# Sparse attention over 2,708 nodes on one Trainium2 core: sum the late rows of h at their pair of q, seven natural tiles and no natural pair

## The chip, the cores and the metric

The kernel runs on one NeuronCore of a Trainium2 chip. The metric is the device time of one execution in microseconds (us); lower is better. Before the change three executions took 743.93, 744.54 and 748.93 us, so the median is 744.54 us. The profiled execution is a further one.

## The reference

`x` is 2708 x 1024, `adj` is a 2708 x 2708 matrix of zeros and ones with a one in about 0.15% of its places (some four per row), the three weights are 1024 x 1024, all float32.

```python
h = jnp.maximum(_layernorm(x, axis=-1), 0.0)
q = h @ W_q.T + b_q
k = h @ W_k.T + b_k
v = h @ W_v.T + b_v
z = (1.0 / math.sqrt(1024)) * (q @ k.T)
spare_z = z * adj
spare_z = jnp.where(spare_z == 0.0, -10000.0, spare_z)
attn = softmax(spare_z, axis=1)
return x + relu(attn @ v)
```

## The kernel before, in words

**The algebra.** The kernel never forms k or v. It multiplies the two weights once into a matrix M, so that a row of `q` (h times M plus a bias) has to be multiplied only with rows of h. For each node it finds its neighbours in `adj`, gathers their rows of h, takes one dot product for each, makes softmax weights of them, and sums the gathered rows into a row u. The output is x + relu(u times W_v plus bias). A node with no edge has equal weights on all nodes, so its u needs the sum of all rows of h (`hsum`).

**Sorting and slots.** Rows are handled in 21 full tiles of 128 rows and a rest of 20. Nodes are sorted by how many neighbours they have, in two parts: the first EARLY tiles, and all others. In a sorted part, tile t needs only K[t] slots (gathers, dot products, sums), from 15 in its first tile to 2 in its last. With EARLY = 9 the slots are 15 7 6 5 4 4 3 3 2 | 15 7 6 6 5 5 4 4 3 3 2 2, in all 111. The tiles that may hold nodes without an edge are EMPTY = (8, 20).

**Stage one** (0 to about 200 us). M is made of 256 matmuls in four parts (`part_of_m`, L340), while ScalarE and VectorE apply the layernorm (`stats`, `root`, `apply`: letters s, r, a in `follow`, L233) and search `adj` (`edges`, L246: letter e). ScalarE's order is written out by hand here: the strings given to `follow` are issued on it in that order, ahead of the evictions that come after them in the code. `apply` also adds each tile to `hsum` on VectorE (L229) and writes it to `h_dram`.

**Natural tiles** (about 128 to 236 us). `query` (L289) forms q of tiles 0 to 6 in natural order, 16 matmuls each. In the middle of tile 4 (`mid`) stands `sort` (L458): two matmuls that count degrees, a few VectorE operations that give every node its place (`pos_i`, L493), and then on GpSimd the writes of one row of a table per node (`put`, L436, one indirect DMA for a tile): first the tiles EARLY to 21, then a load of the sorted table, then two gathers of sorted rows of h (`first_rows`), then the tiles 0 to EARLY - 1, their load, and two more gathers. Tiles 7 and 8 are a natural pair: they are loaded from `h_dram` in order, and `query` of tile 6 stands around their transposes.

**Units.** From here TensorE runs 17 units of two tiles: units 0 to 6 form q of the pairs (7,8), (9,10) to (19,20), units 7 to 16 multiply u with W_v for the pairs in `o_pairs`. A unit is seven products of four matmuls (`multiply`, L754, by a scheme of Strassen's kind with 7 instead of 8 products) and, in between, the 16 transposes of the next unit's rows (`blocks`, L504). VectorE makes four sums s1 to s4 for the next unit (L515) and takes two of the results out of PSUM (L800 and L803 in a q unit, L825 and L829 in an o unit); ScalarE takes out the others.

**The attention stream.** The generator `attention` (L697) yields, tile after tile in the list `order`, dot products (L633), weights (L674 to L677) and sums (L685), all on VectorE in one chain. `advance` weaves it into the units: after each of the seven products, a seventh of 21 us of stream work in a q unit and of 20 in an o unit, from unit 1 on; where the next o unit needs a tile that is not done, the stream is driven on until it is. Gathers go to 13 slots (11 tiles and two that lie in M), first come first served, on GpSimd's queue, which also loads each tile's sorted q (`fetch`, L602), adds x into the result (L815) and scatters it to the output (L598). A tile's u that is not needed within three units is written to `u_dram` and loaded back by SyncE. q of the tiles 0 to 8 lies in `q_dram`, in natural order, and is gathered; that of the others is written sorted, to `q_late`.

Of the kernel before, what the change touches and what calls it, by code (L numbers as in the profile page):

```python
# [26 lines left out]
TW = 18  # L27
ROWS = 7
HIGH = 11
EMPTY = (8, 20)  # L30
EARLY = 9
SINGLE = 7
NONE = 1e-30
FAR = 20.0
WIDE = 8
# [20 lines left out]
def tile_preln_masked_attention(  # L56
# [131 lines left out]
    def stats(group):  # L188

        G = len(group)  # L190
        mv = stat.tile([P, 4, 2], FT, tag="mv", name="mv")
        if tiles[group[-1]][1] < P:
            nc.vector.memset(mv, 1.0)
        xs = []
        for i, t in enumerate(group):
            t0, n = tiles[t]
            xt = row_tile(f"x_{t}")
            nc.sync.dma_start(xt[:n], x[t0:t0 + n, :])
            st = stat.tile([P, NH, 6], FT, tag="st", name="st")
# [21 lines left out]
    def apply():  # L221

        group, xs, r = normed.pop(0)
        for i, t in enumerate(group):
            t0, n = tiles[t]
            xt = xs[i]
            nc.scalar.activation(xt[:n], xt[:n], AF.Relu, bias=r[:n, 4, i:i + 1], scale=r[:n, 3, i:i + 1])  # L227
            nc.gpsimd.dma_start(h_dram[t0:t0 + n, :], xt[:n])  # L228
            nc.vector.tensor_add(hsum[:n], hsum[:n], xt[:n])  # L229

    normed, adj_loads = [], []

# [56 lines left out]
    def query(hT, banks, name, first=False, between=(), mid=None):  # L289

        q = work.tile([P, D], FT, tag="q", name=f"q_{name}", bufs=4)
        order = [(h, c) for h in range(NH) for c in range(DC)]
        if first:

            order.sort(key=lambda hc: hc[1] >= DC // 2)
        for h, c in order:
            if mid is not None and (h, c) == (1, 3):
                mid(mm)
            mm = nc.tensor.matmul(banks[h], hT[:, c, :], M[:, c // 4, h, c % 4, :], start=False,  # L299
                                  stop=(c == DC - 1), skip_group_check=True)  # L300
        for h in range(NH):
            if h < len(between):
                follow(between[h])
            nc.scalar.copy(q[:, h * NB:(h + 1) * NB], banks[h])
        return q

    ordered = ExitStack()
# [2 lines left out]
    with tc.tile_pool(name="w", bufs=1, side="left") as wp:  # L310
# [45 lines left out]
                                     acc[i].rearrange("q (p j c) -> q j c p", j=2, c=4), AF.Copy, scale=scale)  # L356


        follow("s0-3 e0 r e1 a")
        part_of_m(0, 0, "acc")  # L360
        follow("s4-7 e2")
        part_of_m(0, 1, "tp")
        c_sb = row_tile("c_sb")
        for acc_v, dst in ((acc_c, c_sb), (acc_b, bp_sb)):
# [14 lines left out]

        nc.vector.tensor_scalar(large[:, 0:1], large[:, 0:1], 250000.0 / D, None, op0=ALU.is_gt)  # L380
        nc.vector.tensor_scalar(large[:, 1:2], large[:, 1:2], 10000.0, None, op0=ALU.is_gt)
        follow("r e3 a e4 s8-11 e5 r e6 a s12-13 e7 r e8 a")
        part_of_m(1, 0, "tp")
        h_e = {}
        for t in range(2):
# [39 lines left out]

    def first_rows(n):

        rows_of[n + 1] = [row_tile(f"qr_{t}") for t in (EARLY + 2 * n, EARLY + 2 * n + 1)]
        for k, row in enumerate(rows_of[n + 1]):
            last = gather(row, h_dram[:, :], EARLY + 2 * n + k, SLOTS, P)  # L430
        return last

# [99 lines left out]
                    ("e20 e21", ""))  # L532

    in_t = T.rearrange("p k (a c) w -> p k a (c w)", a=2)
    rows_h = list(h_e.values()) + [in_t[:, k, a, :] for k in (2, 1, 3) for a in range(2)][:SINGLE - 2]
# [6 lines left out]
    for t in range(SINGLE):  # L542
        if t + 2 < SINGLE:
            nc.sync.dma_start(rows_h[t + 2], h_dram[(t + 2) * P:(t + 3) * P, :])
        if t + 1 < SINGLE:
            hT[t + 1] = turned(rows_h[t + 1], f"e{t + 1}")
        ahead_banks = seeded(bp_sb) if t + 1 < SINGLE else None
        if t == SINGLE - 1:

            ops_of = {0: blocks(*rows_of.pop(0))}  # L550
            for part in ops_of[0][1:]:
                part()
        q = query(hT.pop(t), banks, f"e{t}", first=(t == 0), between=work_between[t] if t < 4 else (),
                  mid=sort_here if t == 4 else None)
        nc.scalar.dma_start(q_dram[t * P:(t + 1) * P, :], q)
        banks = ahead_banks
        if t == 3:
            search.close()

            att = ph.enter_context(tc.tile_pool(name="att", bufs=1, side="right", reuse_waits="tile"))  # L560
            slots = []
            for i in range(HIGH):
                slots.append(att.tile([P, D], FT, name=f"g{i}"))


            for c in range(4):
                for k, (i, j) in enumerate(((0, 0), (0, 1), (1, 1), (1, 0))):
                    nc.sync.dma_start(slots[2 * c + k // 2][:, k % 2 * NB:(k % 2 + 1) * NB], wv[j][:, i * 4 + c, :])
            for i in range(8, HIGH):
                nc.gpsimd.memset(slots[i], 0.0)  # L570
        if t == 5:
# [80 lines left out]
    def weights(t):  # L652
# [5 lines left out]
        coef = stat.tile([P, SLOTS], FT, tag="coef", name="coef")  # L658
        u = row_tile(f"u_{t}")
        if t in EMPTY:  # L660
            nc.vector.memset(w[:, 0:1], MASKED)
            nc.vector.tensor_scalar(coef[:, :k], ok, -1.0, -MASKED, op0=ALU.add, op1=ALU.mult)
            nc.vector.tensor_mul(w[:, 1:1 + k], z, ok)
# [61 lines left out]
    chain = [behind[-1]]  # L725
    stream = attention(order)
    spent, now = [0.0], [0]

# [56 lines left out]
    def q_results(ta, tb):  # L785
# [1 line left out]
        qb = work.tile([P, D], FT, tag="q", name=f"q_{tb}", bufs=4)  # L787

        def store(q, t):
            dst = q_dram[t * P:(t + 1) * P, :] if t < EARLY else q_late[(t - EARLY) * P:(t - EARLY + 1) * P, :]  # L790
            nc.sync.dma_start(dst, q)
            formed.add(t)
            if t == EARLY - 1:
                formed.update(range(EARLY))

        def c11(X):
            nc.scalar.copy(qa[:, lo], X)
# [2 lines left out]
            nc.vector.tensor_add(qb[:, hi], Y, p5)  # L800

        def c12(Z, u2):
            nc.vector.tensor_add(qa[:, hi], Z, u2)  # L803
            store(qa, ta)

        def c21(Y):
# [53 lines left out]
        return wv[j][:, i * 4:(i + 1) * 4, :]  # L860


    q_pairs = [(t, t + 1) for t in range(SINGLE, FULL, 2)]
    o_pairs = [(6, 7), (5, 0), (4, 3), (9, 2), (8, 1), (10, 11), (12, 13), (14, 15), (16, 17), (20, 18)]
    alone = 19
    units = [("q",) + p for p in q_pairs] + [("o",) + p for p in o_pairs]
    assert alone == order[-1]

    def load_rows(unit):
        kind, *pair = unit  # L870
# [11 lines left out]
        return rows  # L882

    banks_of = {0: banks_for(bp_sb)}

    for h in range(NH):
# [3 lines left out]
    last_q = len(q_pairs) - 1  # L890
    for n, unit in enumerate(units):
        kind, ta, tb = unit
        now[0] = n
        if 1 <= n <= 3:

            i, j = ((0, 0), (1, 0), (1, 1))[n - 1]
            nc.sync.dma_start(m_dram[i, j], M[:, i, j])
        share = (21.0 if kind == "q" else 20.0) / 7
        nxt = units[n + 1] if n + 1 < len(units) else None
        results = (q_results if kind == "q" else o_results)(ta, tb)  # L900

        def after(i):
            if i in (2, 5):
                send()
            if n:
                advance(share)
            if nxt is not None:

                if i == (0 if n else 4):
                    ops_of[n + 1] = blocks(*rows_of.pop(n + 1))  # L910
# [211 lines left out]
```

## Time and profile before

| | |
|---|---|
| median of three executions | 744.54 us (743.93 to 748.93) |
| profiled execution, its own time | 745.27 us |
| its span in the profile | 743.3 us |
| granted TensorE clock, mean of the core | 0.975 |
| VectorE adds to `hsum`, L229, 128 x 1024 | 21, mean 1210 ns |
| dot products L633, 128 x 1024 | 111, mean 1224 ns |
| sums L685, 128 x 1024 | 92, mean 1283 ns |
| gathers of rows of h for slots, L420 on GpSimd | 125, mean 1239 and 1256 ns |
| table writes L440 on GpSimd | 22, mean 1317 ns |
| gathered pair rows `qr`, from issue to landing | 4.2 least, 5.2 median, 9.7 most (us) |

The page gives busy time of each engine, the span in 40 slices, the DMA queues, the chain of work that ended last, the costliest groups with what ended the idle time before them, and the DMA issues with the time to landing. A line such as `xN | busy, mean | idle before <-releaser` names who was waited for. In the timeline of one engine, neighbouring instructions of one kind are merged, the bracket gives the idle time ahead of them, and a float32 matmul leaves two records, so that x8 is one product of four matmuls.

### The profile page before, as it was taken

To read this page: it belongs to the slowest core of one execution; us is meant where nothing else is said; L and a number is where in the kernel's file an instruction comes from. 1 tells how busy PE (TensorE), PEld (TensorE's weight loads), DVE (VectorE), ACT (ScalarE), POOL (GpSimd) and SP (SyncE) were. 2 spreads that over 40 slices of the span, in tenths; PEclk is the share of its full clock that TensorE was granted. 3 is DMA by queue.
4 is the path that set the end of the run, shared out by engine and by line. 5 is a ranking of instruction groups with operands and counts; after the bars stand their busy time and mean duration, and the time that the engine had idled before them with its cause. 6 is when DMAs were issued, how large, how long until landed. Compare 5 with 4: busy or idle time off the path is not lost.

```text
span 743.3 us, 6402 instructions
## 1 busy us (share of the span) xinstructions
PE 689.6 (93%) x1820; PEld 350.4 (47%) x1820; DVE 522.1 (70%) x1068; ACT 254.4 (34%) x381; POOL 306.8 (41%) x281
## 2 busy tenths in 40 slices
PE   7999998999998996899999987999889999999991
PEld 4776765444444442444444433444434444444440
DVE  6978889898891119889999977987889996012001
ACT  0264658587622222321322222332323334222210
POOL 2010111000184764857773652586566862220221
PEclk9999999999999998999999999899899999999997
DMA  9994999999966395788987998899889876631532
GB/s 352 405 403 167 348 402 341 410 399 388 360 218 215 93 378 166 264 309 281 394 315 261 410 414 357 228 346 278 243 265 244 247 222 177 163 51 63 141 73 85
DMA packets 64019, 202.13 MB, mean 272 GB/s; under 512 B 10010, under 2 KB 10362, under 8 KB 62572
## 3 DMA queue, kind: packets, MB, share of 16 engines
q0 software_dynamic: 34736, 109.77, 45.4%
q1 hardware_dynamic: 26940, 84.04, 30.0%
q10 hardware_dynamic: 2304, 7.87, 2.7%
q8 instruction: 16, 0.26, 0.1%
q14 instruction: 23, 0.19, 0.1%
HBM read 166.62 MB, written 48.61 MB: 290 GB/s over the span
## 4 chain that ended last, share of the span: by engine, by line
DMA 19%; PE 15%; issue 15%; POOL 7%; DVE 6%; ACT 1%; POOLq 0%; DVEq 0%
PE ps L744 7%; PE psy L744 7%; DMA g<-h_dram,tab 6%; POOL g L420 4%; DMA out_dram<-y,tab 4%; DMA pq<-q_late 3%; DVE junk L633 3%; DMA y<-in_x_dram,tab 2%; DVE u L685 2%; DMA qr<-h_dram,tab 2%; DMA u_dram<-u 1%; POOL y L815 1%; DMA pq<-q_dram,tab 1%; DVE s L515 1%; PE pt L270 1%
## 5 line engine op out<-in xcount | busy, mean ns | idle before, releaser
L420 POOL DMA_INDIRECT g<-h_dram,tab x107 | 132.6, 1239 | 56.3 <-issue 20.9
L633 DVE SCALAR_TENSOR_TENSOR junk<-g,pq 128x1024 uint8<-128x1024 f32 x94 | 115.0, 1224 | 42.4 <-DMA pq<-q_dram,tab 22.9
L744 PE MATMUL psy<-T,s 128*128 128x512 f32 x272 | 126.3, 608 | 10.6 <-ACT u L768 6.1
L744 PE MATMUL ps<-M,a 128*128 128x512 f32 x272 | 122.3, 592 | 0.0
L347 PE MATMUL ps_m<-wk,wq 128*128 128x512 f32 x256 | 114.2, 608 | 5.3 <-DMA wq<-in_wq_dram 5.3
L685 DVE SCALAR_TENSOR_TENSOR u<-g,coef,u 128x1024 f32<-128x1024 f32 x79 | 101.4, 1283 | 10.3 <-ACT u L677 7.4
L299 PE MATMUL ps<-M,T_e 128*128 128x512 f32 x224 | 97.8, 593 | 0.7 <-ACT ps L286 0.7
L347 PEld LDWEIGHTS ps_m<-wk,wq 128*128 128x128 f32 x256 | 80.2, 314 | 37.4 <-DMA wk<-in_wk_dram 5.3
L744 PEld LDWEIGHTS psy<-T,s 128*128 128x128 f32 x272 | 52.7, 195 | 79.2 <-issue 65.0
L228 POOL DMA_DIRECT2D h_dram<-x x22 | 11.8, 534 | 169.6 <-ACT x L227 169.0
L744 PE MATMUL psy<-T,a 128*128 128x512 f32 x136 | 67.5, 643 | 13.4 <-DVE p L825 12.1
L744 PEld LDWEIGHTS ps<-M,a 128*128 128x128 f32 x272 | 50.5, 190 | 58.1 <-issue 58.1
L255 DVE FIND_INDEX8 at<-ones,adj 128x8 uint32<-128x685 f32 (+1 forms) x88 | 75.8, 865 | 0.0
L299 PEld LDWEIGHTS ps<-M,T_e 128*128 128x128 f32 x224 | 41.9, 190 | 50.7 <-issue 48.8
L744 PE MATMUL ps<-T,s 128*128 128x512 f32 x136 | 61.2, 592 | 0.0
L744 PE MATMUL ps<-M,s 128*128 128x512 f32 x136 | 61.1, 592 | 0.0
L815 POOL DMA_INDIRECT y<-in_x_dram,tab x21 | 36.7, 1749 | 54.9 <-ACT y L830 32.6
L252 ACT ACTIVATE sized<-adj 128x2708 uint8<-128x2708 f32 (+1 forms) x22 | 54.2, 2465 | 2.1 <-DMA adj<-in_adj_dram 2.0
L515 DVE TENSOR_TENSOR s<-a,pt 128x512 f32<-128x512 f32 x34 | 22.0, 683 | 43.0 <-ACT a L511 43.0
L744 PEld LDWEIGHTS psy<-T,a 128*128 128x128 f32 x136 | 27.3, 206 | 51.2 <-issue 31.8
L598 POOL DMA_INDIRECT out_dram<-y,tab x21 | 24.0, 1143 | 64.9 <-DMA y<-in_x_dram,tab 39.2
L744 PEld LDWEIGHTS ps<-M,s 128*128 128x128 f32 x136 | 25.8, 190 | 32.0 <-issue 32.0
(195 smaller groups left out, 719.6 us busy)
## 6 DMA issues: line engine op xcount, KB each, us to landing
adj<-in_adj_dram SPq DMA_DIRECT2D x21, 1354.0 KB, 11.5
x<-in_x_dram SPq DMA_DIRECT2D x21, 512.0 KB, 9.8
h_dram<-x POOLq DMA_DIRECT2D x21, 512.0 KB, 7.7
u_dram<-u POOLq DMA_DIRECT2D x13, 512.0 KB, 6.4
or<-u_dram SPq DMA_DIRECT2D x13, 512.0 KB, 6.2
q_late<-q SPq DMA_DIRECT2D x12, 512.0 KB, 6.4
pq<-q_late POOLq DMA_DIRECT2D x12, 512.0 KB, 5.0
wq<-in_wq_dram SPq DMA_DIRECT2D x8, 512.0 KB, 8.3
```

Source lines behind the costliest of these rows:

```text
L228: nc.gpsimd.dma_start(h_dram[t0:t0 + n, :], xt[:n])
L252: nc.scalar.activation(sized[:n], a[:n, :, :PW], AF.Abs, accum_out=total[:n, t:t + 1])
L255: nc.vector.max_index(at[:n, g, :], ones[:n, 0:8], a[:n, g, :])
L299: mm = nc.tensor.matmul(banks[h], hT[:, c, :], M[:, c // 4, h, c % 4, :], start=False, stop=(c == DC - 1), skip_group_check=True)
L347: nc.tensor.matmul(acc[i], lhs, wk_sb[o][:, cols], start=(o == 0), stop=(o == DC - 1))
L420: return nc.gpsimd.indirect_dma_start(out=dst, out_offset=None, in_=src, in_offset=off, bounds_check=N - 1, oob_is_err=False)
L515: behind.append(nc.vector.tensor_tensor(ops[name], a, b, op=op))
L598: nc.gpsimd.indirect_dma_start(out=out, out_offset=bass.IndirectOffsetOnAxis(ap=ptab.bitcast(U32)[:n, t, SLOTS:SLOTS + 1], axis=0), in_=y[ ...
L633: chained(lambda: nc.vector.scalar_tensor_tensor(junk, g_of[t][s], 1.0, tq[t], op0=ALU.mult, op1=ALU.mult, accum_out=zall[:, t, s:s + 1]))
L685: chained(lambda: nc.vector.scalar_tensor_tensor(u, g_of[t][s], coef[:, at[t][s]:at[t][s] + 1], u, op0=ALU.mult, op1=ALU.add))
L744: nc.tensor.matmul(bank, a[:, c, :], b[:, c, :], start=False, stop=(c == 3), skip_group_check=True)
L815: nc.gpsimd.indirect_dma_start(out=y[:n], out_offset=None, in_=x, in_offset=off, compute_op=ALU.add)
```

## The change

EARLY becomes 7 and SINGLE goes: the sorted parts are tiles 0 to 6 and 7 to 21, and the slots are 15 7 5 5 4 3 2 | 15 8 6 6 5 5 4 4 4 3 3 3 2 2, again 111. EMPTY becomes (6, 20). There is no natural pair: pair (7, 8) is gathered in sorted order like the others. The rows of the tiles 7 to 20 are no longer added to `hsum` in stage one; each pair's gathered rows are added at its unit (`sum_rows`), the rest of 20 rows at unit 1, and the two matmuls with ones that finish the sum (`all_rows`) move from ahead of unit 0 into unit 5. The table of the late part now has 15 writes ahead of it, not 13, and that of the early part 7, not 9.

ScalarE's hand-written order puts each `r` ahead of a search and gives searches to the places between `r` and `a`. One T (the fourth) is made after the v operands. The stream's first step stands in unit 0 and its first work after unit 0; rows for unit 2 are gathered in unit 0; the shares are 18 and 17 us. `order` and `o_pairs` are new, and tile 6, which may hold nodes without an edge, stands 16th. Four tiles of x use another pool tag.

```diff
-EMPTY = (8, 20)
-EARLY = 9
-SINGLE = 7
+EMPTY = (6, 20)
+EARLY = 7
...
-            xt = row_tile(f"x_{t}")
+            if t in (6, 7, 12, 13):
+                xt = work.tile([P, D], FT, tag="q", name=f"x_{t}", bufs=4)
+            else:
+                xt = row_tile(f"x_{t}")
...
-            nc.vector.tensor_add(hsum[:n], hsum[:n], xt[:n])
+            if t < EARLY:
+                nc.vector.tensor_add(hsum[:n], hsum[:n], xt[:n])
...
-        follow("s0-3 e0 r e1 a")
+        follow("s0-3 r e0 a e1")
         part_of_m(0, 0, "acc")
-        follow("s4-7 e2")
+        follow("s4-7 r e2 a e3")
         part_of_m(0, 1, "tp")
...
-        follow("r e3 a e4 s8-11 e5 r e6 a s12-13 e7 r e8 a")
+        follow("s8-11 r e4 a e5 s12-13 e6 r e7 a e8")
         part_of_m(1, 0, "tp")
...
-        rows_of[n + 1] = [row_tile(f"qr_{t}") for t in (EARLY + 2 * n, EARLY + 2 * n + 1)]
-        for k, row in enumerate(rows_of[n + 1]):
+        rows_of[n] = [row_tile(f"qr_{t}") for t in (EARLY + 2 * n, EARLY + 2 * n + 1)]
+        for k, row in enumerate(rows_of[n]):
...
-        if t == SINGLE - 1:
-
-            ops_of = {0: blocks(*rows_of.pop(0))}
-            for part in ops_of[0][1:]:
-                part()
...
-            rows_of[0] = [row_tile(f"h_e{k}") for k in range(SINGLE, EARLY)]
-            for k, row in enumerate(rows_of[0], SINGLE):
-                nc.sync.dma_start(row, h_dram[k * P:(k + 1) * P, :])
...
-        ts_of_m(0, 2, 1, 3)
+        ts_of_m(0, 2, 1)
...
+        ts_of_m(3)
...
+        fill()
+        yield 0.0
...
-    formed = set()
-    order = [6, 7, 5, 0, 4, 3, 9, 2, 8, 1, 10, 11, 12, 13, 14, 15, 16, 17, 18, 20, 19]
+    formed = set(range(EARLY))
+    order = [5, 4, 3, 0, 2, 1, 7, 8, 9, 10, 11, 12, 13, 14, 15, 6, 16, 17, 20, 18, 19]
...
-    for h in range(NH):
-        ps_h = psum.tile([P, NB], FT, tag="tp", name="ps_h")
-        nc.tensor.matmul(ps_h, ones, hsum[:, h * NB:(h + 1) * NB], start=True, stop=True)
-        nc.scalar.copy(hsum[:, h * NB:(h + 1) * NB], ps_h)
+    def sum_rows(rows, n=P):
+        with tc.issue_after(behind[-1].ins):
+            for row in rows:
+                nc.vector.tensor_add(hsum[:n], hsum[:n], row[:n])
...
-        share = (21.0 if kind == "q" else 20.0) / 7
+        share = (18.0 if kind == "q" else 17.0) / 7
...
-            if n:
+            if n == 0 and i == 2:
+
+                next(stream)
...
+            if n or i > 5:
                 advance(share)
...
+                    rows = rows_of.pop(n + 1)
+                    if nxt[0] == "q":
+                        sum_rows(rows)
+                    if n == last_q - 1:
+                        all_rows()
...
-                if i == 4 and n and n + 2 < len(units):
+                if i == 4 and n == 1:
+                    rest = row_tile("h_rest")
+                    gather(rest[:REST], h_dram[:, :], FULL, SLOTS, REST)
+                    sum_rows([rest], REST)
+                if i == 4 and n + 2 < len(units):
```

More of the change, by code (lines that the diff above doesn't have):

```diff
@@ L295, in query, with evict @@
             order.sort(key=lambda hc: hc[1] >= DC // 2)
+        def evict(h):
+            if h < len(between):
+                follow(between[h])
+            nc.scalar.copy(q[:, h * NB:(h + 1) * NB], banks[h])
         for h, c in order:
             if mid is not None and (h, c) == (1, 3):
+                evict(0)
                 mid(mm)
@@ L300, in query @@
                                   stop=(c == DC - 1), skip_group_check=True)
-        for h in range(NH):
-            if h < len(between):
-                follow(between[h])
-            nc.scalar.copy(q[:, h * NB:(h + 1) * NB], banks[h])
+        for h in range(NH) if mid is None else (1,):
+            evict(h)
         return q
@@ L534, in tile_preln_masked_attention @@
     in_t = T.rearrange("p k (a c) w -> p k a (c w)", a=2)
-    rows_h = list(h_e.values()) + [in_t[:, k, a, :] for k in (2, 1, 3) for a in range(2)][:SINGLE - 2]
+    rows_h = list(h_e.values()) + [in_t[:, k, a, :] for k in (2, 1, 3) for a in range(2)][:EARLY - 2]
     placed = []
@@ L540, in sort_here @@
             placed.append(sort())
-    for t in range(SINGLE):
-        if t + 2 < SINGLE:
+    for t in range(EARLY):
+        if t + 2 < EARLY:
             nc.sync.dma_start(rows_h[t + 2], h_dram[(t + 2) * P:(t + 3) * P, :])
-        if t + 1 < SINGLE:
+        if t + 1 < EARLY:
             hT[t + 1] = turned(rows_h[t + 1], f"e{t + 1}")
-        ahead_banks = seeded(bp_sb) if t + 1 < SINGLE else None
-        if t == SINGLE - 1:
-            ops_of = {0: blocks(*rows_of.pop(0))}
-            for part in ops_of[0][1:]:
-                part()
+        ahead_banks = seeded(bp_sb) if t + 1 < EARLY else None
         q = query(hT.pop(t), banks, f"e{t}", first=(t == 0), between=work_between[t] if t < 4 else (),
@@ L660, in weights @@
         if t in EMPTY:
+            assert summed
             nc.vector.memset(w[:, 0:1], MASKED)
@@ L721, in tile_preln_masked_attention @@
     done, held, at, ws, us = set(), {}, {}, {}, {}
-    formed = set()
-    order = [6, 7, 5, 0, 4, 3, 9, 2, 8, 1, 10, 11, 12, 13, 14, 15, 16, 17, 18, 20, 19]
+    formed = set(range(EARLY))
+    order = [5, 4, 3, 0, 2, 1, 7, 8, 9, 10, 11, 12, 13, 14, 15, 6, 16, 17, 20, 18, 19]
     assert sorted(order) == list(range(FULL))
-    chain = [behind[-1]]
+    chain = [placed[0]]
     stream = attention(order)
@@ L789, in store @@
         def store(q, t):
-            dst = q_dram[t * P:(t + 1) * P, :] if t < EARLY else q_late[(t - EARLY) * P:(t - EARLY + 1) * P, :]
-            nc.sync.dma_start(dst, q)
+            nc.sync.dma_start(q_late[(t - EARLY) * P:(t - EARLY + 1) * P, :], q)
             formed.add(t)
-            if t == EARLY - 1:
-                formed.update(range(EARLY))
         def c11(X):
@@ L802, in c12 @@
         def c12(Z, u2):
-            nc.vector.tensor_add(qa[:, hi], Z, u2)
+            behind.append(nc.vector.tensor_add(qa[:, hi], Z, u2))
             store(qa, ta)
@@ L860, in of_wv @@
         return wv[j][:, i * 4:(i + 1) * 4, :]
-    q_pairs = [(t, t + 1) for t in range(SINGLE, FULL, 2)]
-    o_pairs = [(6, 7), (5, 0), (4, 3), (9, 2), (8, 1), (10, 11), (12, 13), (14, 15), (16, 17), (20, 18)]
-    alone = 19
+    q_pairs = [(t, t + 1) for t in range(EARLY, FULL, 2)]
+    o_pairs = [(order[i], order[i + 1]) for i in range(0, FULL - 1, 2)]
+    alone = order[-1]
     units = [("q",) + p for p in q_pairs] + [("o",) + p for p in o_pairs]
-    assert alone == order[-1]
     def load_rows(unit):
@@ L884, in tile_preln_masked_attention, with all_rows @@
     banks_of = {0: banks_for(bp_sb)}
-    for h in range(NH):
-        ps_h = psum.tile([P, NB], FT, tag="tp", name="ps_h")
-        nc.tensor.matmul(ps_h, ones, hsum[:, h * NB:(h + 1) * NB], start=True, stop=True)
-        nc.scalar.copy(hsum[:, h * NB:(h + 1) * NB], ps_h)
     last_q = len(q_pairs) - 1
+    summed = []
+    def sum_rows(rows, n=P):
+        with tc.issue_after(behind[-1].ins):
+            for row in rows:
+                nc.vector.tensor_add(hsum[:n], hsum[:n], row[:n])
+    def all_rows():
+        for h in range(NH):
+            ps_h = psum.tile([P, NB], FT, tag="tp", name="ps_h")
+            nc.tensor.matmul(ps_h, ones, hsum[:, h * NB:(h + 1) * NB], start=True, stop=True)
+            nc.scalar.copy(hsum[:, h * NB:(h + 1) * NB], ps_h)
+        summed.append(True)
+    ops_of = {0: blocks(*rows_of[0])}
+    for part in ops_of[0][1:]:
+        part()
+    sum_rows(rows_of.pop(0))
+    chain.append(behind[-1])
     for n, unit in enumerate(units):
@@ L904, in after @@
                 send()
-            if n:
+            if n == 0 and i == 2:
+                next(stream)
+            if n == 0 and i == 6:
+                chain.append(behind[-1])
+            if n or i > 5:
                 advance(share)
             if nxt is not None:
-                if i == (0 if n else 4):
-                    ops_of[n + 1] = blocks(*rows_of.pop(n + 1))
+                if i == (0 if n else 3):
+                    ops_of[n + 1] = blocks(*rows_of[n + 1])
                     ops_of[n + 1][1]()
```

## The prediction

> **What bounds the kernel now.** I read the page first, then TensorE's timeline from 100 us on, then GpSimd's and VectorE's around 200 to 300 us, then the waits. On the page, the rows of the 40 slices (18.6 us each):
>
> ```profile
> span 743.3 us, 6402 instructions
> ...
> PE 689.6 (93%) x1820; PEld 350.4 (47%) x1820; DVE 522.1 (70%) x1068; ACT 254.4 (34%) x381; POOL 306.8 (41%) x281
> ...
> PE   7999998999998996899999987999889999999991
> ...
> DVE  6978889898891119889999977987889996012001
> ...
> DMA  9994999999966395788987998899889876631532
> ```
>
> TensorE is busy or waiting in order; it lacks 53.7 us in all (743.3 - 689.6). VectorE is full until slice 12 (220 us), almost empty in slices 13 to 15, and full again until 620 us. So two things set the end: TensorE's own work, and in units 2 to 13 VectorE. TensorE's timeline gives the places of the missing time; the bracket is the idle time ahead, with who ended it:
>
> ```profile
> 114.09 1.21 PE L270 MATMUL pt<-ident,h_e 128*128 128x128 f32 x8 [3.29 <-issue]
> 231.30 1.06 PE L270 MATMUL pt<-ident,h_e 128*128 128x128 f32 x8 [1.89 <-DMA h_e<-h_dram]
> 237.37 3.60 PE L744 MATMUL ps<-M,a 128*128 128x512 f32 x8
> 284.90 5.73 PE L744 MATMUL psy<-T,s 128*128 128x512 f32 x8 [6.10 <-ACT u L768]
> 298.36 3.60 PE L744 MATMUL ps<-M,a 128*128 128x512 f32 x8
> 304.49 1.06 PE L270 MATMUL pt<-ident,qr 128*128 128x128 f32 x8 [2.53 <-DMA qr<-h_dram,tab]
> 442.22 5.40 PE L744 MATMUL psy<-T,s 128*128 128x512 f32 x8 [3.29 <-ACT psy L760]
> 464.00 6.63 PE L744 MATMUL psy<-T,a 128*128 128x512 f32 x8 [5.21 <-DVE p L825]
> 522.44 6.42 PE L744 MATMUL psy<-T,a 128*128 128x512 f32 x8 [3.67 <-DVE p L825]
> 637.09 3.60 PE L744 MATMUL ps<-M,a 128*128 128x512 f32 x8
> ```
>
> The lines at 237.37, 298.36 and 637.09 are the starts of units 0, 2 and 14. Units 3 and 4 start at 326.87 and 352.65, so a unit without a wait takes 25.8 us. From unit 14 on nothing waits: 106.2 us to the end, fixed. Units 0 and 1 took 60.99 instead of 51.6 us, units 2 to 13 took 338.7 instead of 309.6.
>
> The hand-over from natural tiles to units hangs on GpSimd's queue and then on VectorE:
>
> ```profile
> 203.78 0.18 DVE L493 CAST pos_i<-deg 128x22 uint32<-128x22 f32 x1
> ...
> 227.31 0.89 POOL L440 DMA_INDIRECT tab_dram<-tab,pos_i  x1 [0.30 <-issue]
> 233.52 1.12 POOL L447 DMA_DIRECT2D tab<-tab_dram  x1 [5.32 <-DMA tab_dram<-tab,pos_i]
> 237.44 1.02 POOL L422 DMA_INDIRECT qr<-h_dram,tab  x1 [2.24 <-DMA tab<-tab_dram]
> 238.77 0.97 POOL L422 DMA_INDIRECT qr<-h_dram,tab  x1 [0.30 <-issue]
> ...
> 280.37 1.23 DVE L633 SCALAR_TENSOR_TENSOR junk<-g,pq 128x1024 uint8<-128x1024 f32 x1 [17.65 <-DMA pq<-q_dram,tab]
> ```
>
> From `pos_i` to the first gathered pair are 34 us of GpSimd's queue; today the natural pair covers them for TensorE. The first dot product starts only at 280.37, because 13 slot gathers stand ahead of the gather of q and that gather needs the natural pair's stores.
>
> **What the Trainium skill says.** "TensorE: Matmul & The Clock Gate", Part 1: The HAM clock gate, says that the array falls to half its clock after an idle window of about 3.4 us and needs about as long of work to come back. This trace agrees: after waits of 3.3 to 6.1 us eight records took 5.40 to 6.63 us, not 3.60. "SBUF — State Buffer", SBUF: two separate sides, says that GpSimd, and with it the descriptors of its DMAs, can be blocked by VectorE on a shared port. Here a table write took 1.50 to 2.83 us until VectorE's subtractions ended at 223 us, and 0.89 to 0.96 after. "DMA: Bandwidth & Descriptors", Issuing engines are not separate DMA queues, says that all issuers share 16 DMA engines. At 405 to 460 us, when SyncE loads the v operands, their share is 1.02 and a gather lands up to 21.9 us after issue (median 6.6).
>
> **Part 1, stage one.** Fifteen adds of 1.21 us leave VectorE (18.2 us), but TensorE waits there only 3.29 us at 114.09 (the eviction L355 stood on ScalarE behind `apply`, which waited 6.81 us for VectorE's r) and about 1.3 us in three small places. With r issued ahead of a search that chain is hidden, and the last evictions of M's third part have six `apply` ahead of them since the part before, not ten. Value: -3.3. Bounds: 0 (e3 now stands ahead of the second part's evictions, which wait on nothing today) and -4.6. The degree matmuls keep their place in TensorE's order, so `pos_i` moves with TensorE, to about 200.5, and no further. The 18 us of VectorE buy nothing else there.
>
> **Part 2, the hand-over.** Two more table writes, at 1.26 us from start to start after VectorE is done: +2.5. So the second gather starts at 238.77 + 2.5 - 3.3 = 238.0 and lands, at the 4.7 us I take between the least (4.2) and the median (5.2), at 242.7. Transposes of 1.04 us and ScalarE's copy follow; the first product starts at 243.8. TensorE's singles without natural transposes, their wait and the two matmuls with ones (2.1, 1.9 and 1.9 us) end near 231.7 - 3.3 = 228.4: a new wait of some 13 us, and a cold start of 2.1 us (5.73 - 3.60). Behind the waiting transposes stands all of TensorE's queue. Unit 0 in effect starts at 245.9 instead of 237.37: +8.5. The price is between +6 and +13 (a gather at 9.7 us).
>
> **Part 3, units 0 and 1.** GpSimd's early part is 7 writes, so its load comes at 252.8 - 3.3, as before or earlier. In the built order then come 2 pair gathers, 3 slots, 2 pair gathers, 1 slot, and then the gather of q: nine issues of 1.3 us, to 262; q has landed by 270 even at the loaded 8 us. VectorE's s1 to s4 for unit 1 (2.7 us) can't start before TensorE has transposed the second row, six products and 1.7 us of transposes after 245.9, at 268.3. So the first dot product starts at about 272.7, not 280.4. The exponential that ScalarE holds ahead of p5 and u2 then ends its wait near 278 instead of 284, just ahead of TensorE: the wait of 6.10, its cold start and 0.76 go. Unit 2 starts at 245.9 + 51.6 = 297.5, against 298.36: -0.9 for parts 1 to 3 together.
>
> **Part 4, units 2 to 13.** VectorE and TensorE are in step: a unit of before holds some 17 stream steps of 1.27 to 1.30 us and 4 us of s1 to s4 and evictions, 26.0 us against 25.8. In the built order the stream has 9 steps done when unit 2's s1 comes, not 5, and one left at unit 14: 5 fewer in between, -6.4; and 11 adds of 1.21 are new there, +13.3. Net +6.9, uncovered: no unit has slack. The two matmuls with ones now stand in unit 5, +1.9, and wait there for the last add, about +1. Waits of before in these units cost 29.1 with their cold starts. Unit 3's gathers now need not wait behind the dots at 295: -2.5. The wait of VectorE on `pq` at 453.6 (5.27 us, a tile of two slots, whose successor's q is asked for too late on a full DMA) has no like, as tiles of 7, 15 and 8 slots stand there: -5.3. Four round trips of u to memory go (9 stores, not 13): 4 MB in and out, some 10 us of the DMA engines at 400 GB/s; GpSimd's waits on landings let a quarter of it through: -2.5. Sum: 6.9 + 2.9 - 10.3 = -0.5.
>
> **Sum.** 743.3 - 0.9 - 0.5 = 741.9 of span; 2.0 us lie around the span today, so 743.9 on the profiled execution's 745.27, and on the median, 0.7 below it, 743.2. I round to 743.0.
>
> **Rivals.** *The waits of the o units go* (faster). If the earlier start and the missing round trips keep GpSimd ahead, units 6 to 13 lose only what VectorE's own work takes. Of the 18.8 us of waits that part 4 leaves, 12 more go: 731. For it: VectorE's waits in these units are mostly on gathers (at 520 and 542 us over 4 us each). Against: GpSimd's scatters (L598) still wait 39.2 us for x and stand ahead of gathers. *Fifteen slots meet the weights* (slower). Tile 7's fifteen dot products now fall in unit 6, and their refetched rows in unit 7, where SyncE loads seven blocks of 1 MB; tile 9 had them a unit earlier. At 1.27 us a row of 0.5 MB asks for the whole 400 GB/s. With half of it left, 7 of the 22 gathers not hidden cost 1.3 us each, and two cold starts 2.5 each: +14, so 757 to 760. It decides from the point where tile 7's gathers start after SyncE's first load. Against: some eight are issued ahead, and fourteen sums on rows already there follow. *The change doesn't do its own work in stage one*: the eviction wait only moves, and the pair lands late: +3.3 and +4.5, so 751.
>
> **Chances.** Forecast 0.48, with its own range 734 to 752; o waits go 0.24; fifteen slots 0.16; stage one fails 0.12. A measurement of this kernel can tell about 1% from no change: 737.1 and 752.0. Faster: 0.24 and a quarter of the forecast's, 0.36. Slower: 0.14 of the fifteen slots, 0.05 of stage one, 0.02 of the forecast: 0.21. Same: 0.43. Range: leaving 0.1 at each end, below 726 and above 758.
>
> **What would show it.** Right: no wait near 110 us; a wait of 11 to 16 us ahead of the first transposes of `qr`, and unit 0's first records slow; the first dot product at 270 to 275; no wait in unit 1; unit 2 at 296 to 300; unit 14 at 630 to 642. Wrong: a unit 0 after 250 (gathers late), a wait over 10 us in units 6 or 7 (fifteen slots), or unit 14 before 628 (o waits gone).

## The result and the profile after

Eight executions of each kernel, in turn on one chip: the changed kernel 737.78 us median (735.54 to 741.83), the kernel before 748.12 (743.93 to 749.61). The ratio is 0.9877 with a 95% interval of 0.9845 to 0.9909 (the quotient of the medians is 0.986): 1.2% faster, clear of no change. The profiled execution took 735.99 us, with a span of 734.2 against 743.3. On another chip the same kernel, run again, had 0.9784 (0.9739 to 0.9828). So ratios from different chips can differ by 1%. Below, times are set against each other only within one series (one chip, shared runs of the kernel before), or stages of traces are compared.

The page of the changed kernel, the same rows as were shown of before:

```profile
span 734.2 us, 6369 instructions
...
PE   7999998999996998999998999996999989999992
...
DMA  9999599999974596768976899888887988531532
```

On TensorE's row the two slices that cover 427 to 464 us, and read 8 and 7 before, are full (unit 7); the slice at 496 us reads 6 (unit 9). TensorE's timeline, at the places that answer to those of before:

```profile
112.84 1.09 PE L273 MATMUL pt<-ident,h_e 128*128 128x128 f32 x8 [1.54 <-issue]
126.97 14.00 PE L308 MATMUL ps<-M,T_e 128*128 128x512 f32 x32 [1.74 <-ACT ps L289]
234.95 1.94 PE L273 MATMUL pt<-ident,qr 128*128 128x128 f32 x8 [5.87 <-DMA qr<-h_dram,tab]
295.46 3.60 PE L747 MATMUL ps<-M,a 128*128 128x512 f32 x8
432.00 3.60 PE L747 MATMUL ps<-M,a 128*128 128x512 f32 x8
458.50 3.60 PE L747 MATMUL ps<-M,a 128*128 128x512 f32 x8
513.69 6.20 PE L747 MATMUL psy<-T,a 128*128 128x512 f32 x8 [5.86 <-DVE p L825]
628.50 3.60 PE L747 MATMUL ps<-M,a 128*128 128x512 f32 x8
```

The starts are those of units 2 (295.46), 7, 8 and 14. A ledger against before: unit 2 starts 2.9 us earlier; units 2 to 6 take 136.5, not 132.7 (+3.9); unit 7 takes 26.5, not 39.4 (-12.9); units 8 to 13 take 170.0, not 166.6 (+3.4); the rest 105.7, not 106.2. All of the gain and more stands in one unit, the first o unit, where no wait over 0.5 us is left. The wait in unit 9 has stayed: 5.86 us, where it was 3.67.

The hand-over, GpSimd's and VectorE's timeline of the changed kernel:

```profile
201.32 2.83 POOL L447 DMA_INDIRECT tab_dram<-tab,pos_i  x1 [9.83 <-DVE pos_i L500]
...
223.59 0.89 POOL L447 DMA_INDIRECT tab_dram<-tab,pos_i  x1 [0.30 <-issue]
226.19 1.18 POOL L454 DMA_DIRECT2D tab<-tab_dram  x1 [1.71 <-DMA tab_dram<-tab,pos_i]
231.66 0.97 POOL L429 DMA_INDIRECT qr<-h_dram,tab  x1 [0.30 <-issue]
...
271.46 1.22 DVE L633 SCALAR_TENSOR_TENSOR junk<-g,pq 128x1024 uint8<-128x1024 f32 x1
```

Fifteen writes took 22.3 us from first to last start, where 13 took 23.1; the wait for the last landing fell from 5.32 to 1.71; the second gather is issued 7.1 us earlier than before, and the first dot product comes 8.9 us earlier.

### The profile page after: what moved, and what is told of

The parts are those of the page before. It is cut to its first block, busy times and chain, and to the rows that moved or that the text cites. A ratio compares the mean times of both kernels' runs of the same rounds, so it can differ in the third digit from the quotient of the medians.

```text
span 734.2 us, 6369 instructions
## 1 busy us (share of the span) xinstructions
PE 685.1 (93%) x1820; PEld 349.9 (48%) x1820; DVE 527.8 (72%) x1067; ACT 251.8 (34%) x380; POOL 302.4 (41%) x280
## 5 line engine op out<-in xcount | busy, mean ns | idle before, releaser
L747 PE MATMUL psy<-T,s 128*128 128x512 f32 x272 | 122.5, 593 | 1.9 <-ACT u L771 1.3
L747 PEld LDWEIGHTS psy<-T,s 128*128 128x128 f32 x272 | 51.4, 190 | 67.2 <-issue 63.6
L815 POOL DMA_INDIRECT y<-in_x_dram,tab x21 | 34.9, 1662 | 56.7 <-ACT y L830 37.0
L747 PEld LDWEIGHTS psy<-T,a 128*128 128x128 f32 x136 | 26.5, 202 | 53.5 <-issue 29.6
L598 POOL DMA_INDIRECT out_dram<-y,tab x21 | 24.3, 1155 | 60.8 <-DMA y<-in_x_dram,tab 31.2
L747 PEld LDWEIGHTS ps<-M,s 128*128 128x128 f32 x136 | 25.8, 190 | 32.5 <-issue 32.3
```

The costliest lines, as they stand in the source:

```text
L598: nc.gpsimd.indirect_dma_start(out=out, out_offset=bass.IndirectOffsetOnAxis(ap=ptab.bitcast(U32)[:n, t, SLOTS:SLOTS + 1], axis=0), in_=y[ ...
L747: nc.tensor.matmul(bank, a[:, c, :], b[:, c, :], start=False, stop=(c == 3), skip_group_check=True)
L815: nc.gpsimd.indirect_dma_start(out=y[:n], out_offset=None, in_=x, in_offset=off, compute_op=ALU.add)
```

## Experiments

Three series of four kernels, each series on one chip. Medians of the kernel before were 742.78, 744.66 and 745.69 us.

**First series. The place of the fourth T.**

```diff
-        ts_of_m(0, 2, 1)
+        ts_of_m(0, 2, 1, 3)
...
-        ts_of_m(3)
```

> The changed kernel with one edit undone: the fourth T is again made ahead of the v operands on VectorE. Theory A (the place of this T sets how fast GpSimd writes the table): the writes are 1.85 to 2.5 us each for longer, the last of 15 starts 3 to 4 us later (226 to 228 instead of 223.6), the wait for the last landing grows from 1.7 towards 5 us because the stores of the v operands also come later, so TensorE's wait ahead of the first transposes of qr is 10 to 13 us instead of 5.9, and the time is 4 to 7 us longer than that of the changed kernel (742 to 745). Rival B (the writes are fast for another reason, such as fewer other DMAs at that time): the last write starts within 1 us of 223.6, the wait stays at 5 to 7 us, the time is within 1.5 us of 737.8.

Measured: 732.1 us, ratio 0.9843 (0.9786 to 0.9900). GpSimd's and TensorE's timeline of this kernel:

```profile
226.19 0.89 POOL L447 DMA_INDIRECT tab_dram<-tab,pos_i  x1 [0.31 <-issue]
228.80 1.18 POOL L454 DMA_DIRECT2D tab<-tab_dram  x1 [1.71 <-DMA tab_dram<-tab,pos_i]
...
237.68 3.84 PE L273 MATMUL pt<-ident,qr 128*128 128x128 f32 x16 [8.77 <-DMA qr<-h_dram,tab]
```

From the first write (201.15) to the last are 25.0 us, against 22.3, and unit 1 starts 67.2 us after the first write, against 63.4. So this kernel loses 2.7 us at the table and 3.8 at unit 1. But 2.2 of the 2.7 are four writes that came 1.80 and not 1.26 us apart, and that rhythm also changes where T stays in place (last section); so the place of T itself is not shown to be the cause. The wait for the landing stayed at 1.71: that part has another cause. The time shows no loss against the relatives in its series.

**ScalarE's old strings in the changed kernel.**

```diff
-        follow("s0-3 r e0 a e1")
+        follow("s0-3 e0 r e1 a")
-        follow("s4-7 r e2 a e3")
+        follow("s4-7 e2")
-        follow("s8-11 r e4 a e5 s12-13 e6 r e7 a e8")
+        follow("r e3 a e4 s8-11 e5 r e6 a s12-13 e7 r e8 a")
```

> The changed kernel with ScalarE's three hand-written strings of before (each search ahead of the r that follows it). Theory of the prediction: a wait of 3.3 us returns near 114 us and the time is 3.3 us longer. Theory after the result (the strings bring 1.4 us only, since a second wait of 1.7 us came at 127 in their place): 1 to 2 us longer, the table's first write at 202.5 to 203 instead of 201.3. Rival (other waits of stage one hide it): within 1 us, first write at 201 to 202.

Measured: 729.41 us, ratio 0.9822 (0.9792 to 0.9852). The first table write of this kernel, in GpSimd's timeline:

```profile
197.10 2.83 POOL L447 DMA_INDIRECT tab_dram<-tab,pos_i  x1 [11.45 <-DVE pos_i L500]
```

It comes 4.2 us earlier than with the new strings (201.32), where all theories had it later or unchanged. (The changed kernel did not run in this series, so the time alone does not show the sign.) TensorE's timeline shows no wait between 100 and 230 us: the waits of 1.54 and 1.74 at 112.84 and 126.97 are made by the new strings. ScalarE's timeline shows how. First the `apply` of two tiles and the evictions of M's third part, with the old strings:

```profile
97.50 2.37 ACT L229 ACTIVATE x<-x,r 128x1024 f32<-128x1024 f32 x2 [2.15 <-DVE r L220]
99.78 2.03 ACT L362 ACTIVATE M<-ps_m 128x512 f32<-128x512 f32 x4
```

and the same in the changed kernel:

```profile
107.44 2.37 ACT L229 ACTIVATE x<-x,r 128x1024 f32<-128x1024 f32 x2 [5.95 <-DVE r L220]
112.16 2.03 ACT L362 ACTIVATE M<-ps_m 128x512 f32<-128x512 f32 x4
```

With the new strings more stands ahead of these evictions, and they come 12 us later.

**All adds to hsum in stage one again** (none at the units, and the gather of the rest of 20 rows left out).

```diff
-            if t < EARLY:
+            if True:
                 nc.vector.tensor_add(hsum[:n], hsum[:n], xt[:n])
...
     def sum_rows(rows, n=P):
-        with tc.issue_after(behind[-1].ins):
-            for row in rows:
-                nc.vector.tensor_add(hsum[:n], hsum[:n], row[:n])
+        return
...
-                    gather(rest[:REST], h_dram[:, :], FULL, SLOTS, REST)
-                    sum_rows([rest], REST)
```

> The changed kernel, but all rows of h are added to hsum in stage one as before, none at the units, and the gather of the rest of 20 rows is left out; the two matmuls with ones stay in unit 5. Theory A (in units 1 to 5 VectorE has no slack, the prediction's term of 1.21 us for an add): the 15 adds that leave the units give back 10 to 18 us there, unit 7 starts 10 us or more earlier, stage one loses 3 us or less; the time falls to 727 to 731. Theory B (TensorE sets the pace in the q units, the adds fill gaps): unit 2 to unit 7 takes 133 to 135 us instead of 136.5, stage one loses 1 to 3 us, the time is within 2 us of 737.8. Rival C (the adds in stage one delay the sort): first table write at 204 to 206, the time 739 to 743.

Measured: 736.23 us, ratio 0.9920 (0.9891 to 0.9948), the slowest of the changed kernel's relatives in its series. First write at 202.13, where five traces without these adds and with the same strings have 201.2 to 202.8: beside the new strings the adds cost stage one nothing that shows. Units 2 to 6 take 135.0 us (136.5 in the changed kernel, 135.6 in its second execution below). So, in the net, the adds cost TensorE 0.6 to 1.5 us in these units, as theory B has it, and theory A falls. But unit 7 takes 35.1 us, which no theory had. VectorE's timeline of this kernel shows the end of the fifteen dot products of tile 7 (the weights that follow them, L675), and what came after:

```profile
402.09 0.17 DVE L675 SCALAR_TENSOR_TENSOR w<-w,keys 128x15 f32<-128x15 f32 x1 [0.28 <-ACT w L649]
...
432.29 1.23 DVE L633 SCALAR_TENSOR_TENSOR junk<-g,pq 128x1024 uint8<-128x1024 f32 x1 [3.10 <-DMA g<-h_dram,tab]
...
435.81 1.23 DVE L633 SCALAR_TENSOR_TENSOR junk<-g,pq 128x1024 uint8<-128x1024 f32 x1 [2.29 <-DMA g<-h_dram,tab]
```

In the changed kernel the same row reads:

```profile
424.67 0.17 DVE L675 SCALAR_TENSOR_TENSOR w<-w,keys 128x15 f32<-128x15 f32 x1
```

SyncE issues the loads of the v operands from 404 to 428 us in this kernel, from 408 to 434 in the changed one. With the adds at the units the stream is 17 to 23 us later (402.09 here, 419.60 and 424.67 in two executions of the changed kernel), and its fifteen dot products, whose rows were mostly gathered before, fall into the loads; without them they are over when the loads begin, and VectorE waits for rows gathered amid the loads.

**The kernel before with two tiles swapped in the order.**

```diff
-    order = [6, 7, 5, 0, 4, 3, 9, 2, 8, 1, 10, ...
+    order = [6, 7, 5, 0, 4, 3, 9, 2, 1, 8, 10, ...
```

> The kernel before with one edit: in the list order the tile of two slots (8) stands behind tile 1, not ahead of it; the pairs of the o units are the same, and all else too. Theory A (the waits in units 6 and 7 of before come from the late request for tile 1's q behind a tile of two slots): VectorE's wait on pq near 454 (5.3 us) and TensorE's waits at 442 and 464 (3.3 and 5.2 us with cold starts of about 2 and 3 us) go; unit 7 takes 27 to 31 us instead of 39.4, and the time is 6 to 12 us below that of before. Rival B (the burst of seven loads of 1 MB makes the waits, whatever tile stands there): unit 7 still takes 36 us or more, the time within 3 us of before.

Measured: 737.38 us, ratio 0.9907 (0.9875 to 0.9939), so 6.9 us (4.5 to 9.3) below before. Unit 7 takes 31.2 us. One of its two waits is left, smaller, in TensorE's timeline:

```profile
455.94 5.22 PE L744 MATMUL psy<-T,a 128*128 128x512 f32 x8 [3.62 <-DVE p L825]
```

VectorE's wait for `pq` near 454 is gone. Theory A holds in the main, though one wait is left and unit 9 takes 34.6 us instead of 32.5. Two numbers swapped in the old kernel give 6.9 us, where the whole change gave 9.2 in its own series and 16.1 in the second series below.

**Second series. The changed kernel again.**

> The changed kernel itself, not edited, once more, beside the runs of this call. Its first trace has two long pauses of ScalarE in unit 1 (at 255 to 265.6 and 266.2 to 272.0 us) with which that unit takes 30.8 us, while three relatives of it with the same code there take 25.8. If the pauses belong to that one execution: unit 1 takes 25.8 us here and the span is some 4 us shorter. If they belong to this kernel's instruction layout: unit 1 takes 30 us or more again. The ratio to the kernel before should be 0.985 to 0.991 either way.

Measured: 729.14 us, ratio 0.9784 (0.9739 to 0.9828), outside the range given for the ratio. Unit 1 takes 25.8 us, unit 2 starts at 291.7 and unit 14 at 623.0. ScalarE's timeline, first of the first trace, then of this one:

```profile
272.02 0.58 ACT L807 COPY q<-psy 128x512 f32<-128x512 f32 x1 [5.87 <-remote]
```

```profile
266.13 0.58 ACT L807 COPY q<-psy 128x512 f32<-128x512 f32 x1 [3.29 <-PE psy L747]
```

The same copy at the end of unit 0 follows its matmuls at once here; in the first trace it came some 7 us after them, and TensorE's waits of 1.32 and 2.31 us in unit 1 hang on it.

**All 21 tiles make the round trip of u through memory**, not 9.

```diff
-        return any(t in unit[1:] for unit in units[:now[0] + 3] if unit[0] == "o")
+        return any(t in unit[1:] for unit in units[:now[0] + 2] if unit[0] == "o")
```

> The changed kernel with the look-ahead for keeping u shortened by a unit, so that all 21 tiles make the round trip through memory, not 9. The prediction gave 0.63 us to each round trip saved. Theory A (round trips cost what the prediction said, and are part of the gain): 12 more cost 6 to 9 us, 744 to 747 on the scale of 737.8 for the changed kernel. Rival B (they are hidden): within 2 us of it.

Measured: 750.53 us, ratio 1.0074 (1.0050 to 1.0099), against 0.9784 in its series: 21.6 us for twelve, 1.8 us each. Neither theory gave so much. TensorE's timeline of this kernel:

```profile
557.34 1.94 PE L273 MATMUL pt<-ident,or 128*128 128x128 f32 x8 [4.53 <-DMA or<-u_dram]
605.23 6.61 PE L747 MATMUL psy<-T,a 128*128 128x512 f32 x8 [7.78 <-DVE p L825]
```

Part of the price is a wait for u itself. Part is VectorE's wait for rows of h that share the DMA engines with u: ahead of the second line VectorE waits 6.91 us for a gathered row.

**Tile 9 (6 slots) ahead of tile 7 (15 slots).**

```diff
-    order = [5, 4, 3, 0, 2, 1, 7, 8, 9, 10, ...
+    order = [5, 4, 3, 0, 2, 1, 9, 7, 8, 10, ...
```

> The changed kernel with tile 9 (6 slots) put ahead of tile 7 (15 slots) in the order, the o pairs following the order. Theory A (tile 7's fifteen dot products cover SyncE's seven loads at 405 to 434 us, because their rows were gathered before and GpSimd gathers almost nothing in that time): the dot products move some 15 us later, gathers fall into the loads, VectorE waits for gathers of h in unit 6 or 7 for 4 us or more in all, units 6 to 8 take 4 to 10 us longer than in the changed kernel (80.6 us together), and the time is 3 to 9 us longer. Rival B (only a tile of two slots ahead of a longer one makes the wait, as in the kernel before): units 6 to 8 take 79 to 82 us, the time within 2 us.

Measured: 720.95 us, ratio 0.9674 (0.9636 to 0.9711), the fastest of all. Both theories missed it: it is 8.2 us faster than the changed kernel in its series. Units 6 to 8 take 77.4 us (three clean units; 78.6 in the changed kernel), and unit 9 takes 27.4 instead of 34.6. VectorE's timeline, the end of the fifteen dot products:

```profile
439.35 0.17 DVE L675 SCALAR_TENSOR_TENSOR w<-w,keys 128x15 f32<-128x15 f32 x1 [0.28 <-ACT w L649]
```

I had taken the loads to end with SyncE's last issue. The DMA engines stay full (370 to 420 GB/s) until about 455 us, so the later place covers more of them, not less. GpSimd's and VectorE's timeline in unit 9 of the changed kernel's second execution show what is gone here:

```profile
489.74 1.30 POOL L598 DMA_INDIRECT out_dram<-y,tab  x1 [4.63 <-DMA y<-in_x_dram,tab]
491.35 1.03 POOL L427 DMA_INDIRECT M<-h_dram,tab  x1 [0.30 <-DVE junk L633]
...
496.68 1.22 DVE L633 SCALAR_TENSOR_TENSOR junk<-M,pq 128x1024 uint8<-128x1024 f32 x1 [3.52 <-DMA M<-h_dram,tab]
```

A scatter waits 4.63 us for x to land, a gather stands behind it, and VectorE waits 3.52 us for its row. In the reordered kernel the like scatter waits 1.95, and VectorE waits for no gather in the o units. These waits are what the new order takes away. That it does so by covering the loads is argued: no run moved the loads themselves, and the new order also changes what GpSimd has to issue around units 8 and 9. Three places of the same fifteen dot products:

| dot products of the late 15-slot tile end at | kernels | unit 7 | unit 9 |
|---|---|---|---|
| 401 to 402 | before and its three relatives; adds in stage one | 31.2 to 39.4 | 26.0 to 34.8 |
| 415 to 425 | changed kernel (twice), T in front, old strings, 21 round trips, larger share | 26.1 to 30.0 | 33.6 to 35.2 |
| 439 to 440 | tile 9 ahead of 7, alone and in two more kernels | 25.8 | 27.4 to 27.5 |

**A larger share in the o units, with the old strings.**

```diff
-        share = (18.0 if kind == "q" else 17.0) / 7
+        share = (18.0 if kind == "q" else 20.0) / 7
```

> The changed kernel with ScalarE's strings of before and a share of 20 instead of 17 us in the o units. The strings alone gave 0.982 of before. Theory A (the stream falls behind with 17 us in the o units, so that it is driven on in a lump at the fourth result of unit 9, where TensorE waits 5 to 6 us for VectorE): with 20 us unit 9 takes 27 to 30 us instead of 34, the ratio is 0.972 to 0.978. Rival B (unit 9 waits because gathers come late, or the last units lose it again): unit 9 takes 32 us or more and the ratio is 0.979 to 0.985.

Measured: 728.71 us, ratio 0.9769 (0.9725 to 0.9812), not told apart from the changed kernel's 0.9784. Unit 9 takes 34.8 us. The ratio lies where theory A had it, but the unit shows rival B's cause, late gathers: VectorE still waits 2.62 and 2.08 us for gathered rows there. The first write is at 198.12 here and 202.25 in the changed kernel, 4.1 us apart; at unit 2 2.2 are left of that, and at unit 14 0.6 (622.4 against 623.0). An earlier start was lost again in the o units.

**Third series. Fewer round trips in the kernel before**: 8, not 13.

```diff
-        return any(t in unit[1:] for unit in units[:now[0] + 3] if unit[0] == "o")
+        return any(t in unit[1:] for unit in units[:now[0] + 4] if unit[0] == "o")
```

> The kernel before with one edit: a tile's u is kept in its buffer if it is needed within four units, not three; 8 tiles make the round trip through memory instead of 13. The prediction's price, 0.63 us for each, gives -3. The price that twelve added round trips had in the changed kernel, 1.8 us each, gives -9. Rival (the added ones only hurt because they came late, in units 10 to 13; the ones of before were stored early and cost nothing): within 2 us of before.

Measured: 739.23 us, ratio 0.9924 (0.9897 to 0.9951): 5.7 us for five, 1.1 each (0.7 to 1.5). It is unit 9 that gets shorter, 26.0 us instead of 32.5 (unit 10 takes 32.3 instead of 28.6), in TensorE's timeline of this kernel:

```profile
494.87 3.60 PE L744 MATMUL ps<-M,a 128*128 128x512 f32 x8
...
520.88 3.60 PE L744 MATMUL ps<-M,a 128*128 128x512 f32 x8
```

**The natural pair's loads earlier in the kernel before** (written at `t == 4`, not `t == 5`).

> The kernel before with the two loads of the natural pair (0.5 MB each) issued by SyncE a tile earlier in the program, ahead of the stores of the v operands and not behind them. Theory (these 1 MB stand in the DMA engines in front of the last table writes, and make the wait of 5.3 us for their landing): the wait ahead of the table's load is 1.5 to 2.5 us, the first gathered pair is issued 3 to 4 us earlier, the time changes by less than 3 us since the natural pair covers it. Rival (the wait comes from the stores of the v operands, or belongs to 13 writes): the wait stays over 4.5 us.

Measured: 745.19 us, ratio 0.9990 (0.9963 to 1.0018). Inconclusive, for the edit moved nothing: in SyncE's and GpSimd's timeline the loads are still issued behind the stores of the v operands, and the wait is there.

```profile
227.14 1.36 SPq L574 DMA_DIRECT2D h_e<-h_dram  x2
...
231.99 1.11 POOL L447 DMA_DIRECT2D tab<-tab_dram  x1 [5.05 <-DMA tab_dram<-tab,pos_i]
```

What is left is the comparison of traces: with a natural pair the wait was 4.95 to 5.50 us in four traces, and the DMA engines are full until about 231 us; without one it was 1.71 to 1.72 in ten, and in the changed kernel the engines fall idle at about 223.

**Old strings and the new order together; and u kept for four units as well.**

> The changed kernel with the old strings for ScalarE (each search ahead of r) and tile 9 ahead of tile 7 in the order. If the two gains add (4.1 us at the first table write, 8 us in units 9 and 12): first write at 197 to 198.5, unit 14 at 610 to 613, ratio to before 0.961 to 0.965. If an earlier start is lost again at a later wait, as it was with the old strings alone (0.9769 with a larger share, against 0.9784): 0.966 to 0.970.

> The kernel of e9_best2 with u kept for four units as well: 6 round trips through memory instead of 10. At 1.8 us each: 7 us less than e9_best2; at 0.63: 2.5 less; if no wait hangs on them once the order is this one: within 1.5 us of it.

Measured: 726.91 us (721.63 to 731.44), ratio 0.9746 (0.9676 to 0.9815), and 724.78, ratio 0.9738 (0.9690 to 0.9787). They are not told apart from each other, so four round trips fewer are worth nothing that shows once the order is this one. In the two traces the gains don't add: the first writes are at 197.42 and 197.70 as expected, but in both ScalarE pauses in unit 1 as in the first trace of the changed kernel, unit 1 takes 33.6 and 33.3 us, and unit 14 starts at 619.8 and 618.5, later than with the new order alone (615.1). Without the pauses, which cost 7.5 to 7.8 us here, the old strings might still pay; that stays open. The lowest ratio measured is that of the new order alone, 0.9674 in the second series; the three were not run side by side, so which of them is best is not shown.

## Why the prediction was right or wrong

The sum, 741.9 us of span, was 7.7 too long: 2.0 in parts 1 to 3, 5.2 in part 4, 0.5 at the end. The range held the time, but from 726 to 758 it would have held the kernel before as well. "Within 1%" was called likelier than "faster". By the mark set there, 737.1, the median of 737.78 is within 1% by a little; against the kernel before in the same series it is 1.2% faster. Luck had a part: unit 0 started 7.0 us earlier than forecast, and ScalarE's pauses in unit 1, which I did not forecast, took 5.0 of them back.

**Part 1, stage one (-3.3).** The size came out (the first write is 2.9 earlier), the reason did not. The step that failed is "With r issued ahead of a search that chain is hidden": the new strings, to which I gave the 3.3, lose 4 us. "The 18 us of VectorE buy nothing else there" holds beside the new strings and is in doubt beside the old ones. The first write's time falls into four groups: kernel before and three relatives (adds kept, old strings) 203.3 to 205.2; adds kept and new strings 202.1; adds gone and new strings 201.2 to 202.8; adds gone and old strings 197.1 to 198.1. From the first group to the last are 5 to 8 us: `apply` waits 2.15 us for r instead of 6.81, and the eviction wait at 114 goes by itself. The new strings then give back 4, most of it in the two waits of 1.5 and 1.7 us. I saw the chain, but credited the edit that was aimed at it.

How much of the 5 to 8 us the adds bring is not shown, for another edit stands in the same comparison: the other pool tag of four tiles of x. A pool tag names the set of buffers that a tile is put in. VectorE's timeline of the kernel before:

```profile
57.78 0.69 DVE L201 BATCH_NORM_STATS2 st<-x 128x6 f32<-128x512 f32 x1 [5.78 <-DMA x<-in_x_dram]
72.63 0.17 DVE L213 RECIPROCAL r<-r 128x4 f32<-128x4 f32 x1
```

and of the changed kernel with the old strings:

```profile
67.39 0.17 DVE L215 RECIPROCAL r<-r 128x4 f32<-128x4 f32 x1
```

Seven buffers hold rows, so in the kernel before the load of the eighth row of x is issued only at 51.56 us, and VectorE waits for it. With the new tag it is issued by 29.7 us in all ten traces, and that wait is gone, also where all adds were kept. So VectorE is 5.2 us ahead at this r, before the first add that was taken away (it stood at 83.18). No run changed the tag alone or the adds alone beside the old strings.

**Part 2, the hand-over (+8.5).** Unit 0 started 1.5 later, not 8.5: outside the bounds. Two terms failed. "+2.5" for two more writes at 1.26 took the other 13 as they were; but the fast ones began with the fourth write, not the tenth, so 15 writes took 0.8 less than 13. (With the same code as before but for two swapped tiles, 13 took 20.4 and not 23.1, so I can't put all of this down to the moved T.) And I carried the landing wait of 5.32 over as fixed, though the change takes away 1 MB of loads that was issued beside the last writes. That cause rests on traces, as told above, and is not shown by a run. The new wait was therefore 5.9 and not 13 us; its cold start (1.94 and 1.88 us for eight transposes instead of 1.04) was as forecast in kind, and agrees with the page that I named there.

**Part 3 (first dot product at 272.7, no wait in unit 1, unit 2 at 297.5).** The first dot product came at 271.5, for the reason given. Without ScalarE's pauses unit 1 has no wait and takes 25.8 us, in seven of ten traces; in the one that the prediction is measured by it took 30.8. Unit 2 at 295.5 and 291.7.

**Part 4 (-0.5).** Measured -5.7 (333.0 against 338.7), and -7.5 in the second execution. Its terms:
- "+13.3, uncovered, no unit has slack": failed. The adds of units 2 to 6 cost TensorE 0.6 to 1.5 us in the net. I set the stream at 17 steps a unit as before, though the diff lowers the share from 21 to 18, which is room for two adds of 1.21 us; no run gave the q units their 21 us back, so this reason is read from the code. What the adds do is to delay the stream by some 20 us, and this helped: unit 7 takes 26.1 to 30.0 us with them and 35.1 without.
- "+2.9" for the matmuls with ones: right in kind, too small. Unit 5 takes 29.8 us, 4.0 above a clean one (5.7 in the second execution), with a wait of 2.03 for the last add.
- "-5.3" for the wait on `pq`: right in cause, too small. The swap in the kernel before took 8.2 us out of unit 7, as the cold starts and waits behind it go too.
- "-2.5" for four round trips: too small by the price measured in two other places, 1.1 and 1.8 us each, so -4.5 to -7; with the new order of tiles four fewer gave nothing that shows. And the unit where it shows in the kernel before (9) still waits in the changed one, for a gather behind a scatter; there no gain shows.

**The rivals.** "Fifteen slots meet the weights" (+14) has the sign reversed: in the traces the dot products of a long tile, their rows gathered ahead, are what best stands beside the loads, and placing them still more squarely there gave another 8.2 us. My "against" sentence held this argument, and I gave it too little weight. "The o waits go" (731) is near to what happened: unit 7's went, unit 9's did not. "The change doesn't do its work in stage one" was half right: the strings didn't; the adds and the new tag together did.

## What to carry to other kernels

When bulk loads are due, look at what the dependent engine will be consuming while the DMA engines are full: work on data that is already there should stand in that window, and short tasks that ask for a fresh row should not. The waits in these traces fit this rule, and a swap in an order list was worth about 1% twice here. Take a change apart by its edits before crediting any: here one of them (the issue order) undid half or more of what two others (fewer adds, and a load that no longer waits for a buffer) had won between them, and one of these I had not priced at all. And work added to an engine costs what its pacing leaves uncovered, which the diff may have changed in the same breath.

## What of the hardware was not expected

Table writes beside 512-wide subtractions of VectorE, which start every 0.60 us, took two rhythms in the same instruction order: 1.80 us from start to start in the trace of before (three subtractions) and 1.26 in that of its relative with two tiles swapped (two, of which one then takes 0.73 and not 0.68). A 2048-wide subtraction of 2.28 us costs a write 1.85 to 2.83. The Trainium skill, "SBUF — State Buffer", SBUF: two separate sides, says that VectorE and GpSimd share a port pair which one instruction holds to its end, a VectorE operation with two inputs in SBUF only against a GpSimd instruction that reads SBUF. The subtractions have two such inputs and the writes read from SBUF, so the slow writes fit this. That the port is the cause is not shown by any run here, and that the rhythm can lock in two ways is only seen here.

ScalarE pauses in unit 1, in 3 of 10 traces of the changed kernel and its relatives, for some 4 to 6 us, with its inputs ready and no work of the program that would explain it in the profile, while slot gathers keep the DMA engines about 90% busy or more, as they also do in traces without a pause. It costs 5 to 8 us. The Trainium skill, "Runtime: NRT & Kernel Launch", Instruction fetch mechanics, says that an engine fetches its instructions by a DMA queue of its own and that this is mostly hidden. The traces have one packet on such a queue a few microseconds ahead of the pauses, but also at the same place where there is no pause; so the cause stays open.
